# A two-layer adaLN block on one core: the first expert block placed in the first stage, and some of layer 1's rows turned by VectorE and transfers

## The chip, the cores and the metric

The kernel runs on one core of one Trainium2 chip. The metric is the device time in microseconds (us) from launch to end; lower is better. Engines are named as the profile names them: PE (TensorE's matmuls), PEld (its weight loads), DVE (VectorE), ACT (ScalarE), POOL (GpSimd) and SP (SyncE, which here only issues transfers).

## The reference

Two transformer layers work on x, 4 batches of 1024 tokens of 256 features, all in float32. In each layer a modulation vector, computed from a small condition `c`, gives shifts, scales and gates.

```python
h = _layernorm(x) * (1 + ca) + sa
x = x + ga * _L0_attn_ref(h, queries, combiners)      # linear attention in 4 heads
h = _layernorm(x) * (1 + cb) + sb
x = x + gb * _L0_ffn_ref(h, W1, b1, W2, b2, Wr, br)   # 8 experts 256 -> 1024 -> 256, top 2
...
h = _layernorm(x) * (1 + ca) + sa
x = x + ga * _L1_attn_ref(h, w0, w1, w2)              # chunks of 128 tokens, one after another
h = _layernorm(x) * (1 + cb) + sb
x = x + gb * _L1_ffn_ref(h, router_w, expert_weights) # 8 experts 256 -> 256, top 2
```

`_L1_attn_ref` runs over 8 chunks (128 tokens of each of the 4 batches). A chunk computes `out = (silu(h a0) * (h a2)) a1`, takes the mean squared difference of `out` and `h` as a loss, and shrinks all three weights by `1 - LR * loss` for the next chunk. So chunk c + 1 needs a number, the decay, that only exists when all of chunk c's outputs do.

## The kernel before

The tokens stay in SBUF as `x_sb`, 128 tokens on the partitions, 8 chunks of 4 batches. Three stages follow one another. Most of the work is recorded as pieces in a `Plan` object: each piece names an engine, a planned duration, what it comes after, which buffers (slots) it holds and a rank. `Plan.run` simulates the engines with those numbers and emits the instructions in the order that it finds. On the chip every engine then works through its own queue in that order. An optional `lag` is time after the instruction until its result counts as there.

**First stage (to about 115 us).** Attention of layer 0, the second normalisation, the router, and the list of blocks. The normalised rows `h` of all tokens go to the DRAM table `h_rows` by SP transfers (`store`), with two numbers per token (`mark`). Every token goes to two experts. The pairs of token and expert are sorted by expert into blocks of 128 rows; there are J = 71 places for blocks. Block 0 always belongs to the last expert, and `first_weights` loads that expert's `W1` and `W2` rows into both buffers of each (`w1buf`, `w2buf`). Which rows a block has is found in three steps: `reach` (DVE) compares, `look` (PE) counts, `find` (DVE) writes the row numbers; `fetch` (POOL) is the indirect DMA that collects them. `begin` makes what block 0 needs for that. The lists of all other blocks need `close_staged` (a chain of small DVE instructions), `across` (PE), `limits` (DVE) and, for the weights, `list_weights` (DVE). `kept_busy` runs matmuls on a constant tile, which compute nothing. Three pieces of layer 1's modulation rows (`modulation1`) are matmuls of low rank.

**Second stage (to about 613 us).** For each block: two gathers of weights (`weights_in`, `weights_out`; rows whose number lies beyond the table are not loaded, which is how a repeated expert is skipped), rows turned so that features are on partitions (`turn_rows`, `rows_turned`), 16 products of `W1` (`hidden`, tile `p_h`), ReLU on ACT (`rectified`), 8 products of `W2` (`values`, tile `p_y`), bias (`biased`) and a scatter to DRAM (`kept`). The loop is written out by hand. In step j PE runs `hidden` of block j, turns the rows of block j + 1, and then runs `values` of block j - 1. From block 12 on, blocks come in fours (quads): four blocks' rows are turned by two DVE transposes, which turn each 32 x 32 square where it lies, into a tile `square`, and 16 SP transfers of 32 KB put the squares where they belong in `xTq` (`quad_turned`).

**Third stage.** Layer 1, again a `Plan`. For each chunk c: `combine` loads layer 0's expert outputs (`yg`) and adds them to x; `normal` of kind "1" makes `h` and its transpose `hT`; `fast` runs the chunk's attention (`p_u`, gate and product into `hf`, `p_f`); `normal` of kind "2" normalises again for the router (`routed`). Chunks 0 to 3 form one group of expert blocks, 4 to 6 another (`block`, tiles `xg`, `xT`, `p_e`, `y`), and chunk 7 is computed for all experts (`dense`). In `normal`, the transpose is eight 128 x 128 PE transposes against `ident` into PSUM (tile `pm_t`) and two ACT copies to `hT`:

```python
m = plan(PE, 0.5, mm, after=hs, holds=[ps, slot], rank=rank - 0.03)
ts.append(plan(ACT, 0.67, out_, after=[m], holds=[ps, slotT], rank=rank - 0.03))
```

The rank of a chunk's kind 1 is c - 1.2, so it is prepared while chunk c - 1 is computed. PE's `p_u` has three PSUM banks (`p1`); `hf` has ten buffers, of which a chunk uses eight.

Of the kernel before, what the change touches and what calls it, by code (L numbers as in the profile page):

```python
# [19 lines left out]
P = 128  # L20
# [3 lines left out]
E = 8  # L24
# [117 lines left out]
def adaln_d2_kernel(  # L142
# [218 lines left out]
    class Pairs:  # L361
# [225 lines left out]
        def close_staged(self, scratch):  # L587


            J, blocks, runs, origin, up1 = self.J, self.blocks, self.runs, self.origin, self.up1  # L590
            begin2 = float(J - LATE)

# [10 lines left out]
            nc.vector.tensor_copy(blocks[:, :, 1:], blocks_i)  # L603
# [304 lines left out]

    plan = Plan(p1=3, p2=2, pm=3, xn1=5, h1T=2, xn2=6, h2T=2, t1=1, le=2)
# [301 lines left out]
    def second_half(b):  # L1211
# [73 lines left out]
        for gs in routed:  # L1285
# [26 lines left out]
            plan("SP", 1.0, mark, after=[d], rank=rank)  # L1312
            for g in gs:
                back, slot, key = backs[g]

                def store(g=g, key=key):
                    at = 4 * g * B * P
                    nc.sync.dma_start(
                        h_rows[at : at + 4 * B * P, :D].rearrange(
                            "(c b p) d -> b p c d", b=B, p=P  # L1320
                        )[b],
                        tiles["xn", key],
                    )

                plan("SP", 4.0, store, after=back, holds=[slot], rank=rank)
# [18 lines left out]
    def first_weights():  # L1344

        for i in range(2):
            nc.sync.dma_start(w1buf[i], W1[(E - 1) * P :, :])
            nc.sync.dma_start(w2buf[i], W2[(E - 1) * P :, :])
        gate_in(1, gb0)
# [26 lines left out]
    for piece in range(3):  # L1376
        ps = plan.slot("p2")
        m = loaded
        for k in range(KD):

            def mm(piece=piece, k=k):
                if k == 0:
                    tiles["rows1", piece] = psum(ps_2, [B, 2 * D], "pm_mod")
                nc.tensor.matmul(
                    tiles["rows1", piece],
                    lhsT=sT1[:, k, :B],
                    rhs=tiles["wm1"][:, k, 2 * D * piece : 2 * D * (piece + 1)],
                    start=(k == 0),
                    stop=(k == KD - 1),
                )  # L1390

            m = plan(PE, 0.87, mm, after=[m, of_batch["routed"]], holds=[ps], rank=20.0)

        def out_(piece=piece):
            modulation1(tiles["rows1", piece], piece)

        plan(ACT, 0.8, out_, after=[m], holds=[ps], rank=20.0)
# [9 lines left out]
    d = plan(DVE, 3.9, lambda: g0.close_staged(pa), after=[m], holds=[ps], rank=-1.0)  # L1407
# [9 lines left out]
    ps = plan.slot("p1")  # L1417
    m = plan(PE, 0.4, lambda: g0.across(ps_1), after=[d], holds=[ps], rank=-1.0)
    kept_busy(1.1, [m], 30.0)
    d = plan(DVE, 1.4, lambda: g0.limits(pa), after=[m, bs], holds=[ps], rank=-1.0)  # L1420
    plan(DVE, 1.2, lambda: g0.list_weights(pa), after=[d], holds=[ps], rank=-0.75)
    for j in range(AHEAD):
        ps = plan.slot("p1")

        def reach(j=j):
            tiles["reached", j] = g0.reach(pa, j)

        def look(j=j):
            tiles["counts", j] = g0.look(ps_1, tiles["reached", j])

        def find(j=j):
            g0.find(pa, tiles["counts", j], j)

        first = -1.0 + 0.1 * j if j else -1.6
        r = plan(DVE, 0.5, reach, after=[d] if j else [begun], rank=first)
        m = plan(PE, 0.25, look, after=[r], holds=[ps], rank=first)
        plan(DVE, 0.6, find, after=[m], holds=[ps], rank=first if j else -0.95)
        if j < AHEAD - 1:
            kept_busy(0.7, [m], 30.0 + j)
    with tc.manual_schedule(engines=ORDERED):  # L1440
# [32 lines left out]
        hf=10,  # L1473
# [93 lines left out]
    def normal(key, c, kind, after, mods, rank, parts):  # L1567
# [5 lines left out]
        for part in parts:  # L1573
# [64 lines left out]
            for b in part:  # L1638
# [17 lines left out]
                hs.append(x)  # L1656
        ts = []
# [20 lines left out]

    def turn_rows(j):
        pt = psum(ps_m, [P, KD, P], "pm_x")  # L1680
        for k in range(KD):
            nc.tensor.transpose(pt[:, k, :], xgbuf[j % 4][:, k:D:KD], ident)
        return pt

    def rows_turned(pt):
        xT = work.tile([P, KD, P], F32, tag="xT", name="xT", bufs=3)
        nc.vector.tensor_copy(xT, pt)  # L1687
        return [xT[:, k, :] for k in range(KD)]

    def in_quads(j):  # L1690
        return 3 * QUAD <= j < turning

    def rows_of_block(j):
        if in_quads(j):
            return xgquad[j // QUAD % 2][:, j % QUAD, :]
        return xgbuf[j % 4]

    def quad_turned(j):

        rows = xgquad[j // QUAD % 2]  # L1700
        square = quads.tile([P, P // SQ, KD, QUAD, SQ], F32, tag="square", name="square", bufs=1)
        for k in range(KD):
            nc.vector.transpose(
                square[:, :, k, :, :].rearrange("p m b s -> p b m s"),
                rows[:, :, k:D:KD].rearrange("p b (m f) -> p b m f", f=SQ),
            )
        xT = quads.tile([P, P // SQ, KD, QUAD, SQ], F32, tag="xTq", name="xTq")
        for q in range(P // SQ):
            for m in range(P // SQ):
                nc.sync.dma_start(  # L1710
                    xT[m * SQ : (m + 1) * SQ, q, :, :, :], square[q * SQ : (q + 1) * SQ, m, :, :, :]
                )
        for b in range(QUAD):
            turned_quads[j + b] = [xT[:, :, k, b, :] for k in range(KD)]
            dests[j + b] = g0.aim(work, rows[:, b, :], j + b)

    def weights_in(j):
        gather(w1buf[j % 2], W1, g0.wrow[:, j : j + 1], E * P - 1)

    def weights_out(j):  # L1720
        gather(w2buf[j % 2], W2, g0.wrow[:, j : j + 1], E * P - 1)

    def hidden(j, xT, m4):
        w1 = w1buf[j % 2]
        p1 = psum(ps_1, [P, 4, P], "p1_h")
        for i in range(4):
            m = 4 * m4 + i
            for k in range(KD):
                nc.tensor.matmul(  # L1729
                    p1[:, i, :],  # L1730
                    lhsT=w1[:, k * H + m * P : k * H + (m + 1) * P],
                    rhs=xT[k],
                    start=(k == 0),
                    stop=(k == KD - 1),
                )
        return p1

    def rectified(j, hid, p1, m4):
        for i in range(4):
            m = 4 * m4 + i  # L1740
            nc.scalar.activation(  # L1741
                hid[:, m, :],
                p1[:, i, :],
                AF.Relu,
                bias=w1buf[j % 2][:, KD * H + m : KD * H + m + 1],
            )

    def values(j, hid):
        w2 = w2buf[j % 2]
        p2 = psum(ps_2, [P, D], "p2_y")  # L1750
        for m in range(KH):
            nc.tensor.matmul(  # L1752
                p2,
                lhsT=hid[:, m, :],
                rhs=w2[:, m * D : (m + 1) * D],
                start=(m == 0),
                stop=(m == KH - 1),
            )
        return p2

    def biased(j, p2):
        y = work.tile([P, D], F32, tag="y", name="y", bufs=3)
        nc.vector.tensor_tensor(y, p2, w2buf[j % 2][:, KH * D :], ALU.add)  # L1763
        return y

    dests, ys0, turned_quads = {}, {}, {}

    def aimed(j):
        dests[j] = g0.aim(work, xgbuf[j % 4], j)

    def kept(j):
        put("g0", dests[j], ys0[j])

    def new_hidden():
        return work.tile([P, KH, P], F32, tag="hid", name="hid")

# [19 lines left out]
    def once(j):  # L1796

        if j in (4, 5):
            gate_of(rows1[:, 3 * j - 10, :], rows1[:, 3 * j - 10, :], work)
        if j == 5:  # L1800
            nc.sync.dma_start(mod_rows1, rows1)
        if j == 6:
            g0.weights(work)
        if 8 <= j < 8 + len(loads):
            nc.sync.dma_start(*loads[j - 8])

    with tc.manual_schedule(engines=ORDERED | {EngineType.SP}):
        looks = {0: (3,), 1: (4,)} | {j: (j + 3, j + 10) for j in range(2, 9)}
        fetches = {j: (j + 2,) for j in range(4)} | {j: (j + 2, j + 8) for j in range(4, 10)}
        for j in range(2):  # L1810
            g0.fetch(rows_of_block(j), h_rows, j)
        xT, hid = rows_turned(turn_rows(0)), None
        aimed(0)
        for j in range(turning):
# [11 lines left out]
            new = new_hidden()  # L1826
            for m4 in range(2):
# [9 lines left out]
            if j:  # L1837
                ys0[j - 1] = biased(j - 1, values(j - 1, hid))
            if j % QUAD == 0 and in_quads(j + QUAD):
                quad_turned(j + QUAD)  # L1840
# [630 lines left out]
    for c in range(NC):  # L2471
# [3 lines left out]
        else:  # L2475
# [14 lines left out]
                ("n1", c), c, "1", [[d] for d in sums], (SHA, SCA), c - 1.2, [range(B)]  # L2490
# [4 lines left out]
            ("n2", c), c, "2", [[d] for d in sums], (SHB, SCB), 7.65 if c == NC - 1 else c + 0.92, [range(B)]  # L2495
# [117 lines left out]
```

## Time and profile before

| | us |
|---|---|
| three runs | 1110.22, 1111.39, 1111.56 (median 1111.39) |
| the profiled execution, its own time | 1111.26 |
| its span, first to last instruction | 1109.5 |
| PE busy in the span | 1067.5 |
| DVE busy | 588.3 |
| ACT busy | 429.6 |
| POOL busy | 423.3 |
| mean granted TensorE clock, share of full speed | 0.991 |

A group of the page names the line, engine, operation and tiles (output, then inputs), how often it ran, its busy time and the mean of one. A timeline line starts with its start in us from the span's start and its length; what released the engine stands in brackets after the idle time. A float32 matmul of the code is two MATMUL records.

### The profile page before, as it was taken

Reading aid. Unit: us, or ns where it says so; the run is one execution under the profiler, and the core shown is the slowest. Engines: PE = TensorE matmul, PEld = TensorE weight load, DVE = VectorE, ACT = ScalarE, POOL = GpSimd, SP = SyncE. Lnnn points to the kernel's source line nnn. Section 1 sums busy time; section 2 is a strip of 40 time slices with the busy share of each in tenths; the row PEclk is TensorE's granted clock in tenths of the full one; section 3 lists DMA queues with packets and bytes.
Section 4 is the critical chain, followed back from the end, with each engine's and each line's share of the span. In section 5 each row is a group of like instructions: output and inputs, shape, how many; then the busy total and the mean of one; then the engine's idle time right before and its main releaser. Section 6 shows DMA issues by size and latency. Waiting matters only on the chain.

```text
span 1109.5 us, 18513 instructions
## 1 busy us (share of the span) xinstructions
PE 1067.5 (96%) x6142; PEld 837.6 (75%) x6142; DVE 588.3 (53%) x2284; ACT 429.6 (39%) x1164; POOL 423.3 (38%) x483
## 2 busy tenths in 40 slices
PE   8998999999999999999999999999999999999894
PEld 5895899998999999999989465665666577656751
DVE  7787343222222222221156488878587535698657
ACT  5977233233332323333344333423325325442531
POOL 2000566555555555554454010110116222743745
PEclk8999999999999999999999999999999999999998
DMA  9404433666552625343071221200004322442544
GB/s 316 190 21 115 154 92 109 246 189 227 170 174 57 214 54 176 98 151 112 20 257 40 73 58 49 72 24 19 1 28 135 95 72 81 128 131 61 170 114 150
DMA packets 86910, 128.69 MB, mean 116 GB/s; under 512 B 30412, under 2 KB 66517, under 8 KB 82206
## 3 DMA queue, kind: packets, MB, share of 16 engines
q0 software_dynamic: 31872, 69.68, 20.1%
q1 hardware_dynamic: 53838, 56.22, 15.9%
q10 hardware_dynamic: 1104, 1.58, 0.4%
q8 instruction: 51, 0.84, 0.3%
q14 instruction: 45, 0.37, 0.1%
HBM read 205.25 MB, written 30.22 MB: 212 GB/s over the span
## 4 chain that ended last, share of the span: by engine, by line
PE 82%; DVE 8%; DMA 6%; ACT 3%; issue 2%; POOL 0%; SPq 0%; DVEq 0%; ACTq 0%; POOLq 0%
PE p_h L1729 20%; PE p_y L1752 20%; PE p_u L2052 19%; PE p_f L2100 10%; PE p_e L2360 4%; DMA w<-in_W,g_wrow 4%; PE pm_x L2343 1%; PE pm_t L1664 1%; DMA xg<-gb_rows,gb_row 1%; PE pm_counts L767 1%; ACT xn L1004 1%; PE pm_b L1071 1%; PE pm_gram L1130 1%; DVE ln_st L978 1%; ACT h2T L1049 1%
## 5 line engine op out<-in xcount | busy, mean ns | idle before, releaser
L1741 ACT ACTIVATE hid<-p_h,w 128x128 f32<-128x128 f32 x544 | 154.9, 367 | 315.1 <-issue 231.7
L1752 PE MATMUL p_y<-w,hid 128*128 128x256 f32 x1088 | 248.8, 382 | 2.5 <-DMA w<-in_W,g_wrow 2.5
L2052 PE MATMUL p_u<-hT,a 128*128 128x512 f32 x512 | 231.6, 596 | 1.1 <-ACTq L2015 0.8
L1752 PEld LDWEIGHTS p_y<-w,hid 128*128 128x128 f32 x1088 | 201.6, 190 | 27.9 <-DMA w<-in_W,g_wrow 3.3
L1729 PEld LDWEIGHTS p_h<-xTq,w 128*128 128x128 f32 x1536 | 179.1, 192 | 2.5
L1729 PE MATMUL p_h<-xTq,w 128*128 128x128 f32 x1536 | 179.2, 275 | 0.0
L2052 PEld LDWEIGHTS p_u<-hT,a 128*128 128x128 f32 x512 | 93.7, 190 | 97.9 <-issue 89.5
L349 POOL DMA_INDIRECT w<-in_W,g_wrow x134 | 135.3, 1009 | 77.2 <-ACT hid L1741 47.6
L1763 DVE TENSOR_TENSOR y<-p_y,w 128x256 f32<-128x256 f32 x68 | 28.9, 424 | 212.6 <-PE p_y L1752 192.7
L814 POOL DMA_INDIRECT y<-y,g_dest x68 | 69.9, 1027 | 133.7 <-DVE g_reached L754 67.3
L2100 PE MATMUL p_f<-a,hf 128*128 128x256 f32 x512 | 116.1, 380 | 0.0
L2100 PEld LDWEIGHTS p_f<-a,hf 128*128 128x128 f32 x512 | 96.1, 190 | 18.0 <-issue 5.9
L2148 POOL TENSOR_TENSOR x_sb<-x_sb,step 128x256 f32<-128x256 f32 x32 | 24.6, 769 | 207.1 <-DVE step L2141 153.7
L780 DVE TENSOR_SCALAR_CACHE_REDUCE g_hits<-pm_counts,g_nth 128x128 f16<-128x128 f32 x68 | 23.6, 348 | 104.2 <-PE pm_counts L767 103.1
L1729 PE MATMUL p_h<-xT,w 128*128 128x128 f32 x640 | 75.1, 276 | 1.5 <-DVE xT L1687 1.5
L1729 PEld LDWEIGHTS p_h<-xT,w 128*128 128x128 f32 x640 | 74.1, 192 | 2.5 <-issue 1.2
L2360 PE MATMUL p_e<-ew,xT 128*128 x280 | 71.1, 386 | 0.3 <-ACT y L2370 0.3
L2064 ACT ACTIVATE hf<-p_u,decay 128x512 f32<-128x512 f32 x56 | 38.2, 684 | 69.2 <-PE p_u L2052 67.0
L349 POOL DMA_INDIRECT xg<-h_rows,g_row x20 | 19.8, 988 | 106.5 <-DVE g_row L789 99.6
L349 POOL DMA_INDIRECT xg<-ga_rows,ga_row x39 | 37.4, 959 | 52.4 <-DVE g_hits L780 17.3
L2360 PEld LDWEIGHTS p_e<-ew,xT 128*128 128x128 f32 x280 | 49.1, 190 | 10.4 <-issue 3.7
L1622 DVE TENSOR_TENSOR h<-h,mod 128x256 f32<-128x256 f32 x128 | 51.5, 425 | 8.9 <-ACT h L1612 6.9
(376 smaller groups left out, 1334.9 us busy)
## 6 DMA issues: line engine op xcount, KB each, us to landing
yg<-y SPq DMA_DIRECT2D x32, 256.0 KB
xTq<-square SPq DMA_DIRECT2D x192, 32.0 KB
ga_y<-y SPq DMA_DIRECT2D x39, 128.0 KB
x_sb<-in_x SPq DMA_DIRECT2D x8, 512.0 KB
h_rows<-xn SPq DMA_DIRECT2D x8, 512.0 KB
gb_y<-y SPq DMA_DIRECT2D x31, 128.0 KB
out_x<-x_sb SPq DMA_DIRECT2D x7, 512.0 KB
a<-in_fw SPq DMA_DIRECT2D x6, 512.0 KB
```

The source lines that it names most:

```text
L349: return nc.gpsimd.indirect_dma_start(out=dst, out_offset=None, in_=table, in_offset=bass.IndirectOffsetOnAxis(ap=index, axis=0), bounds_c ...
L814: nc.gpsimd.indirect_dma_start(out=table, out_offset=bass.IndirectOffsetOnAxis(ap=dest, axis=0), in_=y, in_offset=None, bounds_check=2 * s ...
L1622: nc.vector.tensor_tensor(h, h, mods1[(sc, sh)[i]][:, b, :], (ALU.mult, ALU.add)[i])
L1729: nc.tensor.matmul(p1[:, i, :], lhsT=w1[:, k * H + m * P : k * H + (m + 1) * P], rhs=xT[k], start=(k == 0), stop=(k == KD - 1),)
L1741: nc.scalar.activation(hid[:, m, :], p1[:, i, :], AF.Relu, bias=w1buf[j % 2][:, KD * H + m : KD * H + m + 1],)
L1752: nc.tensor.matmul(p2, lhsT=hid[:, m, :], rhs=w2[:, m * D : (m + 1) * D], start=(m == 0), stop=(m == KH - 1),)
L1763: nc.vector.tensor_tensor(y, p2, w2buf[j % 2][:, KH * D :], ALU.add)
L2052: nc.tensor.matmul(pu, lhsT=a[:, k, m * P : (m + 1) * P], rhs=made["n1", c, "hT"][:, k, :, :], start=(k == 0), stop=(k == KD - 1),)
L2064: nc.scalar.activation(made[key, m], made[key, m, 0], AF.Silu, scale=decays[c])
L2100: nc.tensor.matmul(made[key, "p2", b], lhsT=made[key, m][:, b * P : (b + 1) * P], rhs=a1[:, m, :], start=(m == 0), stop=(m == KH - 1),)
L2148: nc.gpsimd.tensor_tensor(xs, xs, made[key, "step", b], ALU.add)
L2360: nc.tensor.matmul(made[key, "p2"], lhsT=made[key, "xT"][:, k, :], rhs=ew_flat[:, bass.ds(made[key, "at"] + k * D, D)], start=(k == 0), st ...
```

## The change

Block 0 is taken out of the second stage's loop and planned in the first stage. `begin`, `reach`, `look` and `find` of block 0 come first; then `first_block` plans, in this order, the row fetch (POOL), the turning (PE), the copy of the turned rows (ACT, into `xgbuf[3]`, where DVE copied before), `hidden` in four PE pieces of 0.9 us, `rectified` (into `gb0`, used as scratch), and the first half of `values`. The other half of `values` runs in step 0 of the loop, which has no `hidden` any more; step 1 takes block 0's sum from there. Block 1's rows are fetched in the first stage too. `close_staged` loses its first three instructions to `whole_blocks` and is planned after block 0's `find`. The third piece of the modulation rows comes after block 0's `look`. The load of the gate `gb0` moves from `first_weights` to step 3 of the loop. The planned times of the `h_rows` stores on SP change from 1.0 and 4.0 us to 0.4 us and a lag, and block 0's fetch comes after all of them.

In the third stage `normal` gets a flag. With it, two DVE transposes turn the four batches' rows in 32 x 32 squares and sixteen SP transfers move the squares, as `quad_turned` does. Kind 1 has it for chunks 2 to 7, kind 2 for chunks 1 and 2. There is one buffer for the squares, and `hf` has eight buffers instead of ten.

```diff
-    d = plan(DVE, 3.9, lambda: g0.close_staged(pa), after=[m], holds=[ps], rank=-1.0)
+    whole = plan(DVE, 0.45, lambda: g0.whole_blocks(pa), after=[m], holds=[ps], rank=-1.0)
...
-            plan("SP", 1.0, mark, after=[d], rank=rank)
+            stores.append(plan("SP", 0.4, mark, after=[d], rank=rank, lag=1.5))
...
-                plan("SP", 4.0, store, after=back, holds=[slot], rank=rank)
+                stores.append(plan("SP", 0.4, store, after=back, holds=[slot], rank=rank, lag=3.2))
...
-        gate_in(1, gb0)
...
+    def first_block(found):
+        kept0 = tiles["first"] = {
+            "hid": gb0.rearrange("p b d -> p (b d)").rearrange("p (m t) -> p m t", t=P),
+            "xT": xgbuf[3][:, :D].rearrange("p (k t) -> p k t", t=P),
+        }
+        rows = plan(
+            POOL, 1.0, lambda: g0.fetch(xgbuf[0], h_rows, 0), after=[found, *stores], rank=-1.6, lag=2.9
+        )
...
+        m = plan(PE, 0.35, turn, after=[rows], holds=[ps], rank=-1.5)
+        h = plan(ACT, 0.45, lambda: nc.scalar.copy(kept0["xT"], kept0["pt"]), after=[m], holds=[ps], rank=-1.5)
+        done = []
+        for m4 in range(2):
+            ps = plan.slot("p1")
+            for part in range(2):
...
+                h = plan(
+                    PE, 0.9, mm, after=[h], holds=[ps], rank=-0.3
+                )
+            done.append(
+                plan(
+                    ACT,
+                    1.1,
+                    lambda m4=m4: rectified(0, kept0["hid"], kept0[m4], m4),
...
+        def mm():
+            kept0["p2"] = psum(ps_2, [P, D], "p2_y")
+            values(0, kept0["hid"], kept0["p2"], range(4))
+
+        plan(PE, 1.75, mm, after=done[:1], holds=[ps], rank=-0.2)
+
     for j in range(AHEAD):
+        if j == 1:
+            closed = plan(
+                DVE, 2.9, lambda: g0.close_staged(pa), after=[whole, found], rank=-1.0
+            )
...
+            kept_busy(1.0, [m], 30.0)
...
-        first = -1.0 + 0.1 * j if j else -1.6
+        first = -1.3 + 0.4 * j if j else -1.6
...
-        if j < AHEAD - 1:
-            kept_busy(0.7, [m], 30.0 + j)
+        found = plan(DVE, 0.6, find, after=[m], holds=[ps], rank=first)
+        if j == 0:
+            first_block(found)
+        elif j == 1:
+            plan(
+                POOL,
+                1.0,
+                lambda: g0.fetch(xgbuf[1], h_rows, 1),
+                after=[found],
+                rank=-1.5,
+                lag=1.9,
+            )
+        if j == 0:
+            modulation_rows(m, (2,))
+            kept_busy(1.9, [m], 29.0)
...
-        hf=10,
+        hf=8,
+        square=1,
...
+    def turned_by_squares(key, kind, slot, slotT, hs, rank):
...
+            nc.vector.transpose(
+                made[key, "square"][:, :, k, :, :].rearrange("p m b s -> p b m s"),
+                made[*key, "h"][:, :, k * P : (k + 1) * P].rearrange(
+                    "p b (m f) -> p b m f", f=SQ
+                ),
+            )
+
+        def move(q):
+            if q == 0:
+                made[key, "turned"] = buf(f"hT{kind}", [P, P // SQ, KD, B, SQ])
+                made[*key, "hT"] = made[key, "turned"].rearrange("p q k b s -> p k b q s")
+            for m in range(P // SQ):
+                nc.sync.dma_start(
+                    made[key, "turned"][m * SQ : (m + 1) * SQ, q, :, :, :],
+                    made[key, "square"][q * SQ : (q + 1) * SQ, m, :, :, :],
+                )
...
+                    DVE,
+                    0.69,
+                    lambda k=k: transposes(k),
+                    after=d,
+                    holds=[slot, square],
...
+                    SP,
+                    2.6,
+                    lambda q=q: move(q),
+                    after=[*d, *moves[-1:]],
+                    holds=[square, slotT],
+                    rank=rank - 0.03,
+                    lag=2.2 if q == P // SQ - 1 else 0.0,
...
+        if j == 3:
+            gate_in(1, gb0)
...
-        for j in range(2):
-            g0.fetch(rows_of_block(j), h_rows, j)
-        xT, hid = rows_turned(turn_rows(0)), None
+        xT, hid = None, None
...
-            new = new_hidden()
-            for m4 in range(2):
+            new = new_hidden() if j else None
+            for m4 in range(2 if j else 0):
                 rectified(j, new, hidden(j, xT, m4), m4)
...
-            if j:
+            if j == 1:
+                ys0[0] = biased(0, tiles["first"]["p2"])
+            elif j:
                 ys0[j - 1] = biased(j - 1, values(j - 1, hid))
+            if j == 0:
+                values(0, tiles["first"]["hid"], tiles["first"]["p2"], range(4, KH))
...
-                ("n1", c), c, "1", [[d] for d in sums], (SHA, SCA), c - 1.2, [range(B)]
+                ("n1", c), c, "1", [[d] for d in sums], (SHA, SCA), c - 1.2, [range(B)], True
...
-            ("n2", c), c, "2", [[d] for d in sums], (SHB, SCB), 7.65 if c == NC - 1 else c + 0.92, [range(B)]
+            ("n2", c), c, "2", [[d] for d in sums], (SHB, SCB), 7.65 if c == NC - 1 else c + 0.92, [range(B)],
+            c in (1, 2),
```

## The prediction

> **What bounds the kernel now.** I read the page's busy shares and chain first, then the stretches of layer 1 by window, then TensorE's timeline at both places of the change.
>
> ```profile
> PE 1067.5 (96%) x6142; PEld 837.6 (75%) x6142; DVE 588.3 (53%) x2284; ACT 429.6 (39%) x1164; POOL 423.3 (38%) x483
> ...
> PE 82%; DVE 8%; DMA 6%; ACT 3%; issue 2%; POOL 0%; SPq 0%; DVEq 0%; ACTq 0%; POOLq 0%
> ```
>
> TensorE is the bound: 82% of the chain. So an edit is worth what it takes from PE's queue where PE has no gap, or the gap that it fills.
>
> ```profile
> 659.70:703.80 44.10, 44.10 (x165) 26.51 (x164) 39.05 (x124) 18.21 (x41) 3.45 (x5) 1.00 0.22 66
> 703.80:747.90 44.10, 44.10 (x164) 26.53 (x163) 35.75 (x119) 15.68 (x36) 3.01 (x5) 1.00 0.10 31
> ```
>
> Columns: stretch, length, busy PE, PEld, DVE, ACT, POOL, clock, DMA. Two chunks of layer 1: PE has no gap, the clock is full, VectorE has 5 to 8 us left of 44.
>
> ```profile
> 703.92 7.11 PE L2052 MATMUL p_u<-hT,a 128*128 128x512 f32 x16
> 710.87 1.04 PE L1664 MATMUL pm_t<-ident,h 128*128 128x128 f32 x8
> 711.74 8.75 PE L2052 MATMUL p_u<-hT,a 128*128 128x512 f32 x20
> 720.33 1.04 PE L1664 MATMUL pm_t<-ident,h 128*128 128x128 f32 x8
> 721.20 1.88 PE L2052 MATMUL p_u<-hT,a 128*128 128x512 f32 x4
> ...
> 746.20 1.88 PE L2052 MATMUL p_u<-hT,a 128*128 128x512 f32 x4
> ```
>
> A chunk's eight PE transposes push the next p_u back by 0.87 us (710.87 to 711.74). Those at 710.87 serve chunk 3, whose p_u starts only at 746.20.
>
> ```profile
> 110.63 0.48 PE L690 MATMUL pm_blocks<-g_diagonal,ones 128*128 128x142 f32 x2 [1.60 <-DVE g_filled L651]
> ...
> 113.61 0.82 PE L917 MATMUL pm_busy<-busy 128*128 128x512 f16 x3 [0.32 <-DVE g_row L789]
> ...
> 115.80 3.81 PE L1729 MATMUL p_h<-xT,w 128*128 128x128 f32 x32 [1.07 <-DVE xT L1687]
> ...
> 120.37 3.84 PE L1729 MATMUL p_h<-xT,w 128*128 128x128 f32 x32 [0.40 <-DVE xT L1687]
> ...
> 124.39 3.67 PE L1752 MATMUL p_y<-w,hid 128*128 128x256 f32 x16
> ```
>
> The end of the first stage: PE idles or runs fillers while VectorE makes the block lists. Block 0 starts at 115.80, block 1 at 120.37, block 2 (chain) at 128.06.
>
> **Part 1: block 0 in the first stage.** Nothing leaves the useful work; block 0 moves into the gap. With modulation piece 2 behind it, the look of block 0 runs when its reach ends (106.81): 107.2. The three block-count instructions end at 107.4, the find takes 0.54 (110.46 to 111.00): 107.95. POOL starts 0.29 later; rows land 2.93 after that (111.29 to 114.22): 111.2. The stores of h_rows no longer hold it: DMA falls quiet at 107.5. Turning takes 0.3, ScalarE's copy about 0.5 (between its 0.37 for 128x128 and 0.60 for 128x512). Block 0 starts at 112.1, not 115.80.
>
> VectorE's list is half a microsecond later, behind the find: close ends 111.0, across 111.5, limits 112.9, reach 113.35; the look waits in PE's queue behind a piece of block 0 (up to 0.9): 113.9, find 114.5, POOL 114.8, rows of block 1 land at 117.7. PE from 112.1: p_h 3.57, two looks 0.5, about 0.5 that the planner keeps PE free for them, half of p_y 1.75: 118.4. Then turn 0.24, a look 0.25, the other half 1.75 (over block 1's copy): block 1 at 120.65, as before, but p_y of block 0 is done. p_h 3.57, turn 0.24, and 0.51 of copy now bare (as 119.86 to 120.37 is today): block 2 at 124.95. That is **3.1 gained**, and the later blocks keep it: 82% of the chain is PE's, and from 128 to 206 its blocks follow each other without a gap. Ends: 1.0, if rows 1 or W1 of block 2 come late; 5, if the planner wastes nothing. W1 of block 2 is the next to be late: its gather, issued at 121.06 today, landed near 126; behind fetch 1, one gather and fetch 2 it now issues near 118.4 and lands 123.6, 1.3 before it is needed.
>
> At nothing: the two row fetches that move forward on POOL (its queue has been empty for 99.65 us when the first issues today; if it were not, each costs 1.0 of issue on the way to block 0); fillers and modulation piece 2 (same work, in the gap; without the gap 1.7); the 512 KB of gb0, moved on SP to step 3 (SP idle there; first read 400 us later); the stores' planned SP times, 0.4 and a lag for 1.0 and 4.0 (order only, 0.5 either way).
>
> **Part 2: squares.** Eight chunk-rows (n1 of chunks 2 to 7, n2 of 1 and 2) lose their PE transposes: 8 x 0.87 = **7.0**, all in stretches where PE runs on. Their 16 ScalarE copies (0.59 each, 9.4) sat beside PE and gain nothing. Added are two VectorE transposes and sixteen SP moves per chunk, whose rows the second stage already has; the last two lines are SP's queue in time:
>
> ```profile
> L1710 SPq DMA_DIRECT2D xTq<-square x192: 507/589/1742, 182.7 to 512.4; - x192
> ...
> L1703 DVE STREAM_TRANSPOSE square<-xq x24: 668/686/715, 181.3 to 501.8; 128x512 f32<-128x512 f32 x24
> ...
> 182.69 11.04 SPq L1710 DMA_DIRECT2D xTq<-square  x16
> ...
> 726.35 5.66 SPq L1529 DMA_DIRECT2D yg<-y  x2
> ```
>
> The first two lines: name, count, then shortest, median and longest ns. VectorE: 16 x 0.686 = 11.0; the fullest stretch goes to 39.05 + 1.4 = 40.4 of 43.2, so it stays beside PE; were VectorE full, each 1.4 would come onto PE's path. SP: 128 moves, 11 us per chunk. Queued behind them are the yg loads (the last two at 726 to 732) and, from 845, the y stores; the planner counts 10.4 for what takes 11. A store held by 2.6 (one planned group of four moves) keeps one of three y buffers, and p_e then waits; p_u fills in. Rows come 1.4 + 11.0 + about 2 (the landing; estimate from fetch 0's 2.93 less its 1.12 on POOL) = 14.4 after h; the slack is 35 (710.87 to 746.20; 937.8 to 974.9 for chunk 7). n2 of 1 and 2 feeds only the router, whose list closes at 819.
>
> A rule speaks against it. Row: 16 moves in 11.04. The Trainium skill, "DMA: Bandwidth & Descriptors", section "Anatomy of one DMA", puts a fixed cost of about 2.0 us on each transfer, fitted on GpSimd's path. Paid one after another that is 16 x 2.08 = 33 us: chunk 3's rows at 746, level with its p_u, which by then would want them about 4 us earlier; six chunks would give back up to 24, and the sum would be slower by some 14. By the row nothing is given back. I take the row: same engine, shape and size. The other rule, in "VectorE: DVE Perf Modes", "Rules for kernel authors", is to transpose 128x128 on TensorE. It prices an engine by itself; here the row says PE is full and VectorE is not: 7.0 on PE against 1.4 per chunk in a gap.
>
> hf falls from 10 to 8: a chunk needs eight, and the next chunk's first gate waits for the decay, which needs every p_f of this chunk, so all eight are free by then: 0. p_u now reads runs of 32; the page has p_h from xTq at 275 ns and from xT at 276: 0. A new order of the late blocks: 0, within 2 either way (PE idles 1.9 us between 836 and 880, which a luckier order could use and a worse one double).
>
> **Sum.** 3.1 + 7.0 = 10.1 against the profiled 1111.26 (span 1109.5 and 1.8 around it): 1101.2. The median lies 0.13 higher: 1101.3.
>
> **Rivals.** *Block 1 late*: rows or weights of blocks 1 and 2 take block 0's place as the wait. For: its list waits behind a find and PE pieces. Against: 1.3 of margin. Only 7.0 is left: 1104.4. *Half the squares' gain returned* to y stores behind SP's moves and a worse order: 3.1 + 3.5 = 6.6, 1104.8; if more is lost, up to 1109. For: moves of chunks 6 and 7 fall among the late blocks. Against: p_u is there to fill.
>
> *Slower*: VectorE waits for the one square buffer. n1 and n2 follow 9.5 and 11.2 us apart (710.87, 720.33; 753.29, 764.47), but the square is held 14. The planner pushes n2 back, by its own times; if SP's moves run later than planned, VectorE stands at n2's transpose with the hf products behind it, and PE stops when its three p1 banks are full, after 3 x 1.72 = 5.2. At the slowest move seen, 1.742, sixteen take 27.9: 17 over plan, 12 beyond the banks, twice: 24 lost, 14 net, 1125. It decides from 5.05 + 5.2 = 10.2 over plan, 1.3 us per move. Against: the median is 0.589. For: SP's queue is in order and a yg load waits there for its buffer.
>
> That the change doesn't do what it says is unlikely: both pieces of work have rows.
>
> **How the numbers follow.** A measurement here tells about 0.2%, 2.2 us. Both parts as worked out 0.58, block 1 late 0.12, squares half returned 0.10: faster 0.80. The gain eaten by such waits to within 2.2: 0.08. Slower 0.12. Range: 3.1 up to 5 and 7.0 up to 9 with a lucky order give 1097; the high end takes in the rivals, 1109.5. About 0.18 is left above and little below.
>
> **What would show it.** p_h of block 0 near 112 and of block 2 near 125; few fillers after it; pm_t at 64 matmuls, not 128; chunks 0.87 to 1.7 shorter with PE still full; STREAM_TRANSPOSE 16 more, moves 128 more at about 0.6. Wrong if: p_u waits for a DMA of hT, hf products wait behind a transpose, p_u is above 596 ns, or POOL's fetch of block 0 starts after 110.

## The result, and the profile after

The changed kernel takes 1107.02 us (median of nine runs, 1103.51 to 1109.34) against 1111.68 for the kernel before (nine runs beside it): a ratio of 0.9952, 95% interval 0.9937 to 0.9968. That is 4.7 us faster by the medians and 5.3 by the ratio (3.6 to 7.0); the prediction said 10.1 faster, at 1101.3. The direction and the two places were right; about half of the sum arrived.

One warning on how the profile of after must be read: it shows the fastest of its nine runs (1103.51, span 1101.8), 3.5 us below the median. In it the first stage reached the modulation products at 99.64 us, where before needed 101.78. A second profiled execution of the same kernel (after_again below) got there at 101.31. So times in the boundary are counted from that point in each trace, not from the span's start.

The page of after, busy shares and the chain by engine:

```profile
PE 1060.7 (96%) x6079; PEld 829.0 (75%) x6079; DVE 597.5 (54%) x2299; ACT 422.0 (38%) x1149; POOL 422.8 (38%) x483
...
PE 77%; DVE 9%; DMA 7%; ACT 3%; issue 2%; POOL 1%; SPq 0%; DVEq 0%; ACTq 0%; POOLq 0%
```

PE lost 6.8 us of busy time (1067.5 to 1060.7), near the 7.0 of eight turnings. But its share of the chain fell from 82% to 77%, and VectorE and DMA rose: other things end last more often. In this one execution, that is a first sign that removed work has partly become waiting.

The same two chunks of layer 1 by window (stretch, length, then busy PE, PEld, DVE, ACT, POOL, clock, DMA), and TensorE's timeline in the second:

```profile
656.30:699.60 43.30, 43.30 (x156) 25.72 (x155) 37.73 (x120) 16.21 (x37) 3.45 (x5) 1.00 0.24 67
699.60:742.00 42.40, 42.40 (x149) 24.91 (x148) 35.59 (x112) 14.68 (x34) 3.11 (x5) 1.00 0.24 69
```

```profile
699.74 22.56 PE L2185 MATMUL p_u<-hT,a 128*128 128x512 f32 x52
722.14 1.89 PE L2233 MATMUL p_f<-a,hf 128*128 128x256 f32 x8
```

Here the prediction holds: 0.8 less where one turning left, 1.7 less where two did, PE still without a gap, and p_u runs 52 matmuls in one piece where pm_t cut it twice before. The moves and transposes that replace them, with shortest, median and longest ns:

```profile
L1762 SPq DMA_DIRECT2D hT<-square x128: 507/589/1297, 663.9 to 939.8; - x128
L1750 DVE STREAM_TRANSPOSE square<-h x16: 668/704/712, 661.8 to 929.0; 128x512 f32<-128x512 f32 x16
```

The boundary in after, TensorE's timeline:

```profile
107.33 1.90 PE L923 MATMUL pm_busy<-busy 128*128 128x512 f16 x8
...
111.51 0.51 PE L1429 MATMUL pm_x<-ident,xg 128*128 128x128 f32 x2 [0.96 <-DMA xg<-h_rows,g_row]
...
112.48 2.94 PE L1477 MATMUL p_h<-xg,w 128*128 128x128 f32 x24 [0.34 <-ACT xg L1541]
...
120.18 3.73 PE L1477 MATMUL p_h<-xT,w 128*128 128x128 f32 x32
...
124.67 3.84 PE L1477 MATMUL p_h<-xT,w 128*128 128x128 f32 x32 [0.40 <-DVE xT L1434]
```

Blocks 0, 1 and 2 start at 112.48, 120.18 and 124.67, which looks like the predicted 112.1, 120.65 and 124.95. It is not: this execution arrived 2.1 us early. Counted from the modulation products, block 2's p_h comes after 25.0 us; before it was 26.1, and the prediction meant 23.2. Fillers (pm_busy) still stand where PE should have been at work, and the turning waits for the rows' DMA.

### The profile page after: what moved, and what is told of

The parts are those of the page before. It is cut to its first block, busy times and chain, and to the rows that moved or that the text cites. A ratio compares the mean times of both kernels' runs of the same rounds, so it can differ in the third digit from the quotient of the medians.

```text
span 1101.8 us, 18577 instructions
## 1 busy us (share of the span) xinstructions
PE 1060.7 (96%) x6079; PEld 829.0 (75%) x6079; DVE 597.5 (54%) x2299; ACT 422.0 (38%) x1149; POOL 422.8 (38%) x483
## 4 chain that ended last, share of the span: by engine, by line
PE 77%; DVE 9%; DMA 7%; ACT 3%; issue 2%; POOL 1%; SPq 0%; DVEq 0%; ACTq 0%; POOLq 0%
PE p_h L1477 21%; PE p_y L1501 20%; PE p_u L2185 18%; PE p_f L2233 8%; PE p_e L2493 4%; DMA w<-in_W,g_wrow 3%; DVE ln_st L984 1%; PE pm_x L2476 1%; POOL yg L349 1%; DMA xg<-ga_rows,ga_row 1%; PE pm_counts L772 1%; ACT h2T L1055 1%; DVE g_hits L785 1%; ACT xn L1010 1%; DMA xg<-gb_rows,gb_row 1%
## 5 line engine op out<-in xcount | busy, mean ns | idle before, releaser
L1501 PE MATMUL p_y<-w,hid 128*128 128x256 f32 x1072 | 245.0, 382 | 2.4 <-DMA w<-in_W,g_wrow 2.4
L1501 PEld LDWEIGHTS p_y<-w,hid 128*128 128x128 f32 x1072 | 198.7, 190 | 27.0 <-DMA w<-in_W,g_wrow 2.8
L785 DVE TENSOR_SCALAR_CACHE_REDUCE g_hits<-pm_counts,g_nth 128x128 f16<-128x128 f32 x68 | 23.6, 347 | 107.5 <-PE pm_counts L772 101.6
L1477 PE MATMUL p_h<-xT,w 128*128 128x128 f32 x608 | 71.3, 275 | 0.4 <-DVE xT L1434 0.4
L1477 PEld LDWEIGHTS p_h<-xT,w 128*128 128x128 f32 x608 | 70.4, 192 | 1.2 <-DVE xT L1434 0.6
```

The lines of the kernel that those rows point to most:

```text
L785: nc.vector.tensor_scalar(passed, pc[:, :P], self.nth[:, j : j + 1], -float(P), ALU.is_le, ALU.add, accum_out=hits,)
L1477: nc.tensor.matmul(p1[:, i, :], lhsT=w1[:, k * H + m * P : k * H + (m + 1) * P], rhs=xT[k], start=(k == 0), stop=(k == KD - 1),)
L1501: nc.tensor.matmul(p2, lhsT=hid[:, m, :], rhs=w2[:, m * D : (m + 1) * D], start=(m == 0), stop=(m == KH - 1),)
```

## The experiments

Each kernel is compared by ratio with runs of before on its own chip (medians 1112.94 for the first four, 1110.92 for the next four, 1112.43 for the last four). "Spread" is an edit of the study: loads for layer 1 come at every second block.

| kernel | block 0 in first stage | turnings by squares | loads | median, us | ratio to before |
|---|---|---|---|---|---|
| after_again | yes | 8 | as before | 1107.44 | 0.9956 (0.9944 to 0.9968) |
| first_only | yes | 0 | as before | 1113.01 | 1.0008 (0.9995 to 1.0021) |
| squares_only | no | 8 | as before | 1108.94 | 0.9966 (0.9952 to 0.9980) |
| no_store_wait | yes, other rows | 8 | as before | 1106.36 | 0.9943 (0.9925 to 0.9960) |
| before_spread | no | 0 | spread | 1108.66 | 0.9979 (0.9970 to 0.9988) |
| first_spread | yes | 0 | spread | 1105.90 | 0.9952 (0.9937 to 0.9967) |
| after_spread | yes | 8 | spread | 1101.76 | 0.9917 (0.9900 to 0.9934) |
| squares_to_5 | yes | 6 | as before | 1104.77 | 0.9945 (0.9926 to 0.9964) |
| six_spread | yes | 6 | spread | 1101.89 | 0.9898 (0.9876 to 0.9919) |
| seven_spread | yes | 7 | spread | 1101.56 | 0.9894 (0.9874 to 0.9915) |
| six_no_store_wait | yes, other rows | 6 | spread | 1102.71 | 0.9900 (0.9878 to 0.9922) |
| hf8_spread | no | 0, `hf` 8 | spread | 1108.60 | 0.9960 (0.9942 to 0.9978) |

**The same kernel again (after_again).** No edit.

> The changed kernel once more, for a second trace. Open is why its nine runs spread from 1103.5 to 1109.3 us, and why its profiled execution reached the modulation matmuls 2.1 us earlier than before's did (99.64 against 101.78), ahead of all that the change touches. Theory A: the start is a matter of the execution (the granted clock between 18 and 30 us was 0.56, 0.59, 1.00 in the one and 0.53, 0.50, 0.69 in the other); then the modulation matmuls move again by a microsecond or more in this trace, with that clock, and the median stays near 1107. Theory B: the change shortened the first stage itself; then they come at 99.6 again.

The profiled execution took 1106.46 and reached the modulation products at 101.31, block 2 at 125.85: 24.5 us later. The early start of the first profile was that execution's own; the 1.6 us less between there and block 2 (26.1 before) are the change's: the four profiled kernels without block 0 in the first stage have 26.1 to 26.2 us there, the ten with it 23.9 to 25.0.

**Block 0 in the first stage alone (first_only).** After, with TensorE's turnings and ten `hf` buffers.

```diff
-                ("n1", c), c, "1", [[d] for d in sums], (SHA, SCA), c - 1.2, [range(B)], True
+                ("n1", c), c, "1", [[d] for d in sums], (SHA, SCA), c - 1.2, [range(B)]
...
-            c in (1, 2),
...
-        hf=8,
+        hf=10,
```

> Only the first part: block 0 in the first stage, PE transposes everywhere, hf at ten. From the changed kernel's trace the first part gains 1.2 us between the modulation matmuls and block 2 (25.03 us against 26.28), because the row fetch of block 0 starts 2.4 us after its row numbers are there. Theory: 1.2 gained, some 1110.3 us, ratio 0.999, and block 2 some 25.0 us after the first modulation matmul. Rival (the prediction's sum): 3.1 gained, 1108.4.

No gain at all in the median, against either expectation. Yet block 2 starts 24.4 us after the modulation products, 1.7 less than before. So the boundary did get shorter, and something took it back. What follows at 207 us shows where, first before, then first_only (TensorE's timeline):

```profile
206.35 0.28 PE L767 MATMUL pm_counts<-g_more,g_reached 128*128 128x129 f16 x2
207.67 3.72 PE L1752 MATMUL p_y<-w,hid 128*128 128x256 f32 x16 [1.03 <-DMA w<-in_W,g_wrow]
```

```profile
204.49 0.28 PE L772 MATMUL pm_counts<-g_more,g_reached 128*128 128x129 f16 x2
206.93 5.41 PE L1501 MATMUL p_y<-w,hid 128*128 128x256 f32 x16 [2.16 <-DMA w<-in_W,g_wrow]
```

PE arrives 1.9 us earlier, and waits 1.1 longer for a gather of weights. After that the same 16 matmuls take 5.41 instead of 3.72; the window around them has a granted clock of 0.91:

```profile
200.00:220.00 20.00, 17.84 (x112) 16.18 (x111) 4.76 (x20) 4.56 (x16) 8.02 (x8) 0.91 0.55 202
```

**The squares alone (squares_only).** Before, with `turned_by_squares`, its flags and `hf=8`.

```diff
-        hf=10,
+        hf=8,
+        square=1,
...
+        if squares:
+            return slot, slotT, hs, turned_by_squares(key, kind, slot, slotT, hs, rank)
```

> Only the second part: the squares and hf at eight, on the kernel before. Theory: the eight groups of PE transposes leave PE's queue and 0.87 us each comes back as long as PE runs on: 5.5 us by the loss of chunk 6 and about 4 at the end, since the late blocks of the second group lost 1.6 us again in the changed kernel's trace: some 1107 us. Rival 1 (the prediction's sum): 7.0, 1104.5. Rival 2: the moves hold up SP and nothing is left: 1111.

4.0 us by the medians, where 7.0 were predicted. In its trace chunk 0's loss (its `pm_loss` matmuls) to chunk 6's takes 312.2 us (317.0 before), but the way from chunk 6's loss to the dense part (the first `p_e` on chunk 7's `hT`) takes 91.0 (88.6 before): about 5 gained, 2.4 given back behind it. Of the 2.4, 1.1 return by the end: from the start of the dense part on there are four matmul records less (65 instead of 69), for more of the late blocks' work stands ahead of it, and 43.1 us remain instead of 44.2.

**Block 0's fetch without the stores (no_store_wait).** Block 0's gather reads the input's rows, which are not the rows wanted, and waits for nothing that SyncE writes.

```diff
-            POOL, 1.0, lambda: g0.fetch(xgbuf[0], h_rows, 0), after=[found, *stores], rank=-1.6, lag=2.9
+            POOL, 1.0, lambda: gather(xgbuf[0][:, :D], x_in.rearrange("b s d -> (b s) d"), g0.row[:, 0:1], B * S - 1), after=[found, *stores], rank=-1.6, lag=2.9
...
+            if j == 1: g0.fetch(xgbuf[0], h_rows, 0)
```

> The changed kernel, but block 0's rows in the first stage are collected from the input x instead of from the table of normalised rows, so that this fetch needn't wait for the table's stores; its destinations are fetched again in step 1. Block 0's rows are other rows than wanted. Theory: the fetch of block 0 waited for the stores (it started 3.2 us after their last packets and 2.4 us after the find); then it starts about 0.3 us after the find here, block 0 starts 2 us earlier after the list's start, and block 2 some 1.5 to 2 us earlier: 1105 where the changed kernel has 1107. Rival: POOL waited for VectorE or for its own start; then the fetch starts as late as in the changed kernel and nothing is gained.

The fetch on GpSimd and the row numbers it needs on VectorE, first in after, then here:

```profile
106.02 0.16 DVE L794 SCALAR_TENSOR_TENSOR g_row<-pm_counts,g_count 128x1 int32<-128x1 f32 x1
...
108.57 1.13 POOL L349 DMA_INDIRECT xg<-h_rows,g_row  x1 [97.58 <-DVE g_picked L646]
```

```profile
108.10 0.16 DVE L794 SCALAR_TENSOR_TENSOR g_row<-pm_counts,g_count 128x1 int32<-128x1 f32 x1
...
108.54 1.19 POOL L349 DMA_INDIRECT xg<-in_x,g_row  x1 [97.03 <-DVE g_up L611]
```

With the stores in front, the gather starts 2.4 us after its numbers are ready; without them 0.3. The name in brackets in after misleads: `g_picked` is no input of this gather; the stores are what is left, and the DMA engines had gone quiet at 105.5. So a gather that depends on them started 3.1 us after their last traffic.

The eight profiles with the stores in front agree on this (2.8 to 3.3), but not on what it costs, for the stores end at 105.5 to 107.0 whether TensorE reaches the modulation products early or late: 5.9 us behind them in after, 4.0 in first_spread. So the gather starts from 0.4 us (first_spread) to 2.4 us (after) behind its numbers, and block 2 from 23.9 to 25.0 us behind the modulation products; in after_again it is 24.5, here 24.0. The wait cost block 2 between nothing and about 1 us, by the execution.

No more was to be had here, for block 0 then waits for VectorE's lists: its p_h comes after a `pm_counts` that waits for `g_reached`. In time, 1106.36 against 1107.44 with overlapping intervals: not resolved.

**The loads spread (before_spread, first_spread, after_spread).** What was different at 207 us? Before, SyncE's queue:

```profile
182.69 11.04 SPq L1710 DMA_DIRECT2D xTq<-square  x16
193.77 2.57 SPq L1805 DMA_DIRECT2D a<-in_fw  x4
```

`once` issues one load for layer 1 per block, but SyncE's queue is in order: the four pile up behind 16 moves of squares, and leave together, 2 MB just when the blocks' weights are gathered. The edit, the same in all three:

```diff
-        if 8 <= j < 8 + len(loads):
-            nc.sync.dma_start(*loads[j - 8])
+        if j % 2 == 0 and 8 <= j < 8 + 2 * len(loads):
+            nc.sync.dma_start(*loads[j // 2 - 4])
```

> Before, with one edit: the 16 loads for layer 1 that SyncE issues one per block from block 8 (512 KB each) come at every second block, from block 8 to 38. In the trace of before, four of them leave SyncE in 2.6 us at 193.8, behind 16 moves of turned squares, and TensorE then waits 1.03 us for a gather of weights at 207.7; after the group at 253.7 it waits 1.1 us at 258.6 and 266.7. Theory W, the gathers of weights share the DMA engines with these bursts: with bursts half as large the waits of 2.1 us in 125 to 300 shrink to under 0.7, and the time falls by 1.0 to 1.8 us against before. Rival, the gathers are late by their own issue on GpSimd: waits and time stay.

> Part 1 alone (block 0 in the first stage), with the 16 loads at every second block. In first_only the blocks started 1.9 us earlier after the boundary, but the wait for weights at 207 had grown from 1.03 to 2.16 us, and the gain was gone by then. Theory W, part 1's gain runs into gathers that the burst of loads holds back: with the burst halved the gain reaches the end, and this kernel is 1.0 to 1.9 us faster than before_spread, 2.5 to 3.5 faster than before. Rival R, the gain is lost elsewhere, or is not there: this kernel equals before_spread within 0.5 us.

> After, with the 16 loads at every second block. Theory W: the waits of 2.7 us for weights at 206.7 and 265.7 shrink to under 1 us, and the time is 1.5 to 2.5 us below the 1107.4 of after_again. Rival R: the waits stay or come back later, time as after_again within 0.7 us.

before_spread gains 2.3 us, first_spread 5.0, after_spread 9.2. The waits of TensorE between 125 and 300 us, in first_only and in first_spread (total, times, longest):

```profile
PE p_y L1501 <- DMA w<-in_W,g_wrow: 3.5, 2, 2.2
PE p_h L1477 <- DVE xT L1434: 0.4, 1, 0.4
```

```profile
PE p_h L1477 <- DVE xT L1434: 0.4, 1, 0.4
```

The waits for weights are gone, and the half clock behind them with them (after_spread keeps one wait of 0.2 us, seven_spread below one of 0.6). In SyncE's queue two loads now follow each group of moves (192.10, two in 1.05 us). GpSimd issues the gathers of weights ahead of 207 us at the same times in both (198.90 and 203.14 in first_only, 199.21 and 203.45 in first_spread), so it was not their issue that was late.

Part 1 is worth 2.8 us here (first_spread under before_spread: 1108.66 less 1105.90; the intervals of the two ratios just miss each other), where first_only under before was worth nothing. That is more than theory W expected (1.0 to 1.9); the rival, that the gain is lost elsewhere or never there, falls. after_spread lies 5.7 below after_again by the medians, where up to 2.5 were expected; each was run beside other runs of before, and by their ratios it is 0.0039, 4.3 us. Why the spreading is worth more there than the waits seen in one profile each (2.7, and 5.2 in first_only with the slow matmuls), no run settles.

**Fewer turnings by squares (squares_to_5, six_spread, seven_spread).** The flag of kind 1 becomes `c < 6` in the first two, `c < 7` in the third; six_spread and seven_spread also have the loads spread.

```diff
-                ("n1", c), c, "1", [[d] for d in sums], (SHA, SCA), c - 1.2, [range(B)], True
+                ("n1", c), c, "1", [[d] for d in sums], (SHA, SCA), c - 1.2, [range(B)], c < 6
```

> After, but the first normalisation's rows of chunks 6 and 7 are turned on TensorE again: six turnings by squares instead of eight. From the loss of chunk 6 to the start of the dense part before takes 88.6 us, first_only 88.7, the kernels with eight turnings 90.3 to 91.5. Theory L, the two late turnings disturb the order of the late blocks, and give back what they save: that stretch takes 88.7 again, the loss of chunk 6 comes about 1 us later than in after_again, and the time is equal or up to 1 us lower. Rival, the stretch is longer for another reason (the turned rows of chunks 1 to 5): it stays at 90 or more, and the time is 1.0 to 1.7 us above after_again.

> After, with the 16 loads at every second block and six turnings by squares (the first normalisation's rows of chunks 6 and 7 on TensorE again). Theory: the two gains add: after_spread was 9.2 us below before, and without the two late turnings 1.3 to 2.5 us more are won in the late blocks (from the loss of chunk 6 to the dense part 87.7 instead of 91.2, by the loss of chunk 6 1.6 later), so 10.5 to 11.7 below before. Rival, the late stretch is set by something that moves with the time of arrival: no more than after_spread's 9.2.

> As six_spread, but chunk 6's first rows are turned by squares too, so only chunk 7's are on TensorE. It tells which of the two late turnings costs. If chunk 7's alone pushes the late blocks behind the loss of chunk 6, that stretch takes about 87.7 and the kernel is 0.5 to 0.9 us below six_spread; if chunk 6's does, the stretch takes 90 to 91 and the kernel is 1 to 2 us above it.

From chunk 6's loss to the dense part: 87.7 us in squares_to_5, 87.9 in six_spread, 87.7 in seven_spread, against 91.2 in after_spread and 88.2 in first_spread. So theory L has the place right, and of the two late turnings it is chunk 7's that lengthens this stretch: all five profiles with eight turnings need 90.3 to 93.6 us, the nine others 87.7 to 88.7. Chunk 7's saves 0.7 just before chunk 6's loss (46.8 instead of 47.5), and the stretch behind it is 3.5 longer. The two stretches, in after_spread and in seven_spread:

```profile
920.20:967.00 46.80, 46.24 (x178) 29.16 (x177) 33.79 (x100) 19.77 (x45) 17.62 (x19) 1.00 0.35 104
967.00:1058.20 91.20, 84.33 (x402) 56.82 (x403) 69.20 (x300) 39.68 (x104) 48.88 (x52) 1.00 0.47 133
```

```profile
920.40:967.90 47.50, 47.00 (x186) 29.99 (x185) 34.89 (x104) 22.39 (x50) 24.53 (x27) 1.00 0.39 119
967.90:1055.60 87.70, 82.59 (x399) 56.31 (x399) 65.83 (x294) 37.22 (x100) 42.05 (x45) 1.00 0.42 121
```

Not all of the 3.5 are lost. PE is busy for 1.7 more in that stretch (84.33 and 82.59), in part with work of the late blocks that seven_spread does behind the start of the dense part; from there to the end after_spread needs 43.2 us, seven_spread 44.4. From chunk 0's loss to the end they take 445.4 and 444.5, so between these two traces chunk 7's turning costs about 1 us net. Single profiles scatter as much: the four with six or seven turnings lie at 444.5 to 445.8, the five with eight at 445.4 to 450.0.

Read the POOL column, the fifth engine: with chunk 7 on squares it has 19 instructions in the first stretch instead of 27, and the missing ones come behind chunk 6's loss. They are the gathers of group a's expert outputs. after's SyncE queue shows what they wait for, and GpSimd's queue the first of them, in after and then in after_spread, where the bracket names the stores:

```profile
896.18 32.73 SPq L2506 DMA_DIRECT2D ga_y<-y  x15
929.70 10.66 SPq L1762 DMA_DIRECT2D hT<-square  x16
940.78 0.80 SPq L2506 DMA_DIRECT2D ga_y<-y  x2
```

```profile
944.30 0.97 POOL L349 DMA_INDIRECT yg<-ga_y,ga_slot  x1 [24.49 <-issue]
...
943.69 0.96 POOL L349 DMA_INDIRECT yg<-ga_y,ga_slot  x1 [24.67 <-DMA ga_y<-y]
```

The last two stores of `ga_y` stand behind 16 moves, so the gathers begin 23.6 us before chunk 6's loss (967.88). In seven_spread they begin at 935.01, 32.9 us before its loss at 967.92; in first_spread also 32.9. That these 9.3 us on GpSimd are what lengthens the late blocks fits the counts but was not tested by itself; the order of those blocks changed with it, and its share was not separated.

In time the three do not say as much. six_spread and seven_spread are 10.5 and 10.9 us below before, after_spread 9.2, squares_to_5 6.2 and after_again 5.5; the intervals of neighbours overlap. seven_spread has the lowest median and ratio of all, 0.9894 (0.9874 to 0.9915), and its interval lies wholly below that of after, 0.9952 (0.9937 to 0.9968).

**Stores and buffers (six_no_store_wait, hf8_spread).** six_spread with block 0's rows from the input as above, and before_spread with `hf=8`.

> As six_spread, with block 0's rows gathered from the kernel's input instead of the rows that the first stage stores, so that this gather waits for no store (block 0's own rows are gathered once more in step 1 for what comes later). In no_store_wait the blocks started 0.5 us earlier after the boundary than in after_again, and the wait for weights at 207 took it back. Theory: with the loads spread it stays: 0.5 to 1.0 us below six_spread. Rival: the routing's own chain on VectorE and TensorE ends last: within 0.3 us of six_spread.

> before_spread with the ring of hf buffers at 8 instead of 10: the one buffer edit that the change made. The order of VectorE's and TensorE's instructions is the same as in before_spread. Theory: the two buffers were slack, time within 0.5 us of before_spread (2.3 us below before). Rival: they account for part of the squares' missing gain: 1 us or more above before_spread.

six_no_store_wait is not faster than six_spread (1102.71, 1101.89). Block 2 starts 0.6 us earlier after the modulation products (23.95 against 24.57), but a later turning waits 1.3 us for its rows (at 137.9; 0.3 in six_spread), behind the gather that this kernel adds in step 1. So the edit returned its own gain, and what the store wait costs in time stays open.

hf8_spread is no slower than before_spread: the medians are 1108.60 and 1108.66, and by the ratios, each on its own chip, it lies 2.1 us lower (0.9960 and 0.9979, overlapping intervals). The 1 us or more that the rival asked for is not there: the two buffers were slack.

## Why the prediction was right or wrong

**Part 1, 3.1.** The mechanism was right and its size nearly: 2.8 us by the medians once the loads are spread, of which 2.1 are there when block 2 starts (26.15 us after the modulation products in before_spread, 24.04 in first_spread). With the loads as they were it was worth nothing in the median of first_only. Two steps failed.

- "The stores of h_rows no longer hold it: DMA falls quiet at 107.5." They did hold it. I took the end of the DMA traffic for the end of the wait. In after GpSimd started 2.4 us after its numbers; without stores, 0.3, as predicted (0.29). The cost at block 2 was between nothing and about 1 us, by the execution. The prediction's own sign for such a wait, a fetch after 110, lay 1.8 us behind the start that it had worked out (108.2), too late to show it. Even without the stores block 2 comes 24.0 us after the modulation products, not 23.2, since in PE's queue `pm_blocks` and fillers stand ahead of the turning (112.50 in no_store_wait), and the look behind it waits for VectorE.
- "The later blocks keep it: from 128 to 206 its blocks follow each other without a gap." The sentence stops one microsecond short of where the gain ended. The trace of before had a wait for weights of 1.03 at 207.67, and two more by 267: where PE waits for a transfer, an earlier PE waits longer. Blocks 1 and 2, which the rival "Block 1 late" suspected, had their rows and weights in time: TensorE waits for neither there (block 1 starts at 120.18 without a wait).

**Part 2, 7.0.** The unit was right: 0.87 for one turning. By chunk 6's loss, first_spread needs 316.9 from chunk 0's loss and after_spread 311.1: 5.8 of 7.0. The first two stretches between losses gave 0.87 for one turning and 1.76 for two; each later one gave less (1.45 for two, then 0.54, 0.53 and 0.68 for one each). In the one between the losses of 3 and 4 the block list of group a (`pm_blocks`) waits 0.8 for VectorE; why the others fall short no run settles. Behind chunk 6's loss 3.0 were lost up to the dense part (91.2 against 88.2), and 1.1 of them came back behind its start (43.2 against 44.3). So 4.0 remain from chunk 0's loss to the end in these two traces, and 4.1 by their kernels' medians.

The failed term is "a new order of the late blocks: 0, within 2 either way", and with it the SP paragraph: it named the y stores behind the moves from 845 on, took them for one planned group of four moves, 2.6 us, and let p_u fill in. All 16 moves stood ahead of the last two stores, 10.7 us, and the wait that the traces show there is not p_e's but that of the gathers on GpSimd behind those stores. This is the rival "half the squares' gain returned"; it had been given 0.10.

**The slower rival** fell: nobody waits for `square`, and the longest move took 1.30 us, against a median of 0.59.

**The rule on transfers.** Sixteen moves left SyncE in 10.7 us for chunk 7, as the row said; the 33 us that a fixed cost of about 2.0 us (the Trainium skill, "DMA: Bandwidth & Descriptors", "Anatomy of one DMA") would give if paid one after another are excluded. The rule to transpose 128x128 on TensorE, from "VectorE: DVE Perf Modes", lost where PE had no gap (0.87 for each turning up to chunk 2's loss) and held for chunk 7, whose squares cost more elsewhere than they saved (about 1 us net between two traces; the times do not resolve it).

**At nothing.** `hf` from 10 to 8: no cost seen in hf8_spread. The strided `hT`: p_u took 595 ns, 596 before.

**The sum.** 3.1 and 7.0 were added as if they were lengths of one path. What arrived in the kernel as changed, by the medians: 0 to 1.5 of the first (before to first_only; squares_only to after_again), 4 to 5.6 of the second (before to squares_only; first_only to after_again). The interval of the result, 3.6 to 7.0, takes in the rival with 3.1 and 3.5 in it (6.6), but that would be luck: in the rival part 1 stayed whole.

## What to carry to other kernels

A gain on the bounding engine can be lost at the next place where that engine waits for a transfer, as here at 207 us: read every wait behind the edit, not only the stretch after it, and ask what else is on the DMA engines then. In SyncE's queue, loads "one per step" bunched up behind each group of 16 moves, and the moves that were added were paid by the stores that stood behind them; look for who waits for that, on every engine. Before adding a new piece of work everywhere, try it place by place: here one of eight seems to have cost more than it saved.

## What the runs showed of the hardware

- A gather that depends on stores to the same table started 3.1 us after the stores' last traffic (105.5 to 108.57 in after; 2.8 to 3.3 in the eight profiles that have it), and 0.3 us after its numbers when it depended on none.
- After some waits TensorE's clock was granted at half. Behind waits of 1.98, 2.16 and 2.31 us for weights (squares_to_5, first_only, squares_only) sixteen p_y took 5.30 to 5.41 us instead of 3.72; behind waits of up to 1.7 us they took 3.72. Before the last four p_e it is not so plain: after a wait of 3.04 they took 3.75 us in after, 1.95 in squares_only; after one of 2.00, 3.34 in seven_spread, 1.96 in first_only.
- The first stage showed the same without any change in the code around it. TensorE's window from 98 to 100 us in before and in first_only, with the same small waits ahead of it:

```profile
98.00:100.00 2.00, 1.62 (x20) 1.14 (x22) 1.70 (x9) 1.66 (x4) 0.00 (x0) 1.00 0.13 2
```

```profile
98.00:100.00 2.00, 2.00 (x22) 1.29 (x21) 0.39 (x3) 1.23 (x4) 0.00 (x0) 0.50 0.04 13
```

The clock is 1.00 and 0.50. In first_only the matmuls from 97.52 to the modulation products took 4.0 us, the same ones in before (99.24 to 101.78, also at 1.00) 2.5. The half clock shows in that place in five of the profiles, all of kernels with block 0 in the first stage (ten have it there), and in none of the four others: too few to say whether the change has to do with it. Single profiles of this kernel therefore differ by a few us in ways that no edit explains, and the boundary had to be measured from a point behind it.
